# Lists of three groups made beside the scan, a term added by VectorE, and a check moved, in a four-layer graph network on one core

## The chip, the cores and the metric

The kernel runs on one core of a Trainium2 chip. The metric is the device time of one execution in microseconds (us). Five engines work from queues of their own, each strictly in order: TensorE (PE, matrix products), VectorE (DVE), ScalarE (ACT), GpSimd (POOL) and SyncE (SP, which here only starts transfers). They wait for one another through semaphores. Besides the engines 16 DMA engines move data; in this kernel SP starts the large transfers, and POOL the gathers, in which each of 128 partitions fetches a row or an element at an address of its own.

## The reference

A stack of four graph layers over 4096 nodes with 128 features each. `adj` is a 4096 x 4096 matrix that is mostly zeros: a diagonal, and off it entries of 0.05 to 1 with a probability that falls with the indices, so that the first rows and columns (the hubs) hold many more than the others.

```python
# h = relu(layernorm(x)) ahead of each layer; x = x + layer(h, adj) after it
L0: h @ W_self.T + (adj @ h) @ W_neigh.T + b
L1: h @ w[0] + (adj @ h) @ w[1] + (2 * adj @ (adj @ h) - h) @ w[2] + bias
L2: H = h @ weight.T                       # attention along adj.T
    C = alpha_src[None, :] + alpha_dst[:, None]
    Tau = adj.T * exp(max(0.2 * C, C))
    Z = (adj.T * (Tau / Tau.sum(axis=1, keepdims=True))) @ H
L3: s = h @ msg_w[:, :D].T
    d = h @ msg_w[:, D:].T
    messages = gelu(s[:, None, :] + d[None, :, :] + msg_b)
    aggregated = einsum('ijd,ij->id', messages, adj)
    new = concat([h, aggregated]) @ upd_w.T + upd_b
    g = gelu(new) + h
    out = layernorm(g) * ln_w + ln_b
```

Layer 3 needs one message per nonzero entry of `adj` and no more, since an entry of zero takes its message away.

## The kernel before

**Order of the work.** The kernel is written as tasks: Python generators that yield what they need next, an engine with a guessed duration (`yield "DVE", 0.35 * n`), a buffer out of a set (`yield banks`), or an event (`yield here[q]`). `Plan.run` goes through them at build time: it keeps a clock for each engine, takes the task that could begin first, among those within a short patience the one of the lowest rank, and emits its instructions. What it emits is the order of each engine's queue; on the chip the semaphores decide the times, and no engine overtakes in its queue. A guessed duration of PE is multiplied by `PE_TIME` = 0.72 before it is added to the clock. Where the planner sees a gap on PE it emits products of a tile of nothing (`fill`, L609), into a PSUM bank that is idle.

**Stages.** In the profiled execution: from 0 to about 373 us a *scan* reads all of `adj`, 128 rows at a time, and marks in bit masks which entries are nonzero (ACT makes an fp8 mask, DVE packs it into words and picks out candidates with `max8`); layer 0 runs beside it. Dense parts near the hubs are multiplied as whole blocks (`big`, L1138), the rest through rows that POOL gathers from tables in DRAM (`g`, L553) and PE multiplies (L1155). Layer 0's products end at 422 us. Layer 1 follows to 637, layer 2's first half to 904, the attention runs from 891 to 1245, layer 3 from there to 1524. `finish_0(g)` closes layer 0 for a group of 4 blocks of 128 rows (g from 0 to 7) and writes the next layer's input, a `norm`, into `hB[:, blocks, :128]`; hB has 32 x 130 columns.

**Lists of entries.** Layer 3 works on *chunks* of up to 128 nonzero entries, 158 in all, made by `entries(number, group)` for 11 groups of units. Group 0 is two hub units with 12 chunks; groups 1 and 2 have 7 each; groups 3 to 10 have 26, 22, 18, 16, 14, 12, 12 and 12. A pass waits for the scan's candidates of its units (`picked`), takes a lane of scratch tiles, decodes the bit marks on DVE, builds selection matrices (`selection`: ACT L622, DVE L624), multiplies them with the running counts (PE, L883 and L884), copies the product (ACT, `ehit`, L887), compares (DVE, L890) and unpacks row, column and address (`e_row`, `e_col`, `e_at`). Then it sets `decoded[number]`. `values()` waits for one group after the other and lets POOL gather the entries' values, one indirect DMA for each chunk (`e_val` from `adj`, L553). In the program before, these tasks are started when the scan is done (two lanes in the pool `second`); the first pass begins at 424.6 us, the last ends at 931.7; the first value gather is issued at 608.3, the last near 1170.

**Layer 3.** `Messages` has for each group g of 4 blocks a `prepare(g)` (own message of the diagonal), and for each batch of up to 4 chunks a `rows` task, which has POOL gather the rows of d (`m`, `tau` and `e` are the tiles' names, L553), and a `message` task: `selection` (L622, L624), the matrices r on DVE (L1400), a wait for the gathered rows, on PE a product of the identity with them (L1406, which adds d into PSUM) and products that add s (L1408), GELU from PSUM on ACT (L1412), and a product that sums into the accumulator (L1418). `finish(g)` makes the update, the layer norm (L1438 to L1459) and the last three DVE steps: times ln_w (L1463), plus ln_b (L1464), plus x (L1465), and has SP write the rows out.

**Check.** A dense version of the whole network stands behind the sparse one. After layer 3, written behind the last `plan.run()` and so behind everything in the queues, 79 small DVE instructions and one product (L1623 to L1646) look whether any list was too short for its entries; `n_bad` is loaded by every engine (L1648), and a branch (L1655) runs the dense version where it isn't 0. With these inputs it is 0.

Of the kernel before, what the change touches and what calls it, by code (L numbers as in the profile page):

```python
# [12 lines left out]
F32 = mybir.dt.float32  # L13
F8 = mybir.dt.float8e4
BF16 = mybir.dt.bfloat16
F16 = mybir.dt.float16
# [238 lines left out]
class Plan:  # L255
# [10 lines left out]
    PATIENCE = 0.3  # L266
    PE_TIME = 0.72
# [31 lines left out]
    def run(self, until=lambda: False):  # L299
        while self.tasks and not until():  # L300
# [32 lines left out]
            duration = want[1]  # L333
            if want[0] == "PE":
                duration *= self.PE_TIME
                gap = begin - self.free["PE"]
                if self.filler and gap > self.SHORT:
                    self.filler(self.free["PE"], gap * self.FILLED)
# [40 lines left out]
def sparse_stack(tc, x, adj, adjT, diag, w_self, w_neigh, b0, w1, b1, w2, att_src, att_dst,  # L379
# [8 lines left out]
    plan = Plan()  # L388
    EARLY = 7
    with ExitStack() as ctx:  # L390
# [7 lines left out]
        def kept(name, shape, dtype=F32):  # L398
            return keep.tile(list(shape), dtype, name=name, tag=name)
# [12 lines left out]
        def by_block(v, n):  # L412

            return v[:, None, :].to_broadcast([P, n, D])
# [189 lines left out]
        def fill(begin, time):  # L604

            idle = min((free, i, slots.items) for slots in (banks, picks) for free, i in slots.free + [(1e9, 0)])
# [198 lines left out]
        def entries(number, group):  # L805
# [178 lines left out]
        def finish_0(g, agg):  # L984
            blocks = slice(g * GB, (g + 1) * GB)
            rows = xN[:, blocks, :]
            p = yield banks
            yield "PE", 8 * 0.42
            times(p, GB, [(hT[:, g * BANK:(g + 1) * BANK], w_self_sb), (agg, w_neigh_sb)])
            plan.release(aggs, agg)  # L990
            yield on_dve(BANK)
            nc.vector.tensor_add(rows, rows, rows_of(p))
            plan.release(banks, p)
            yield from norm(blocks, hB[:, blocks, :D])
            h1_done[g].set(plan.finish)
# [320 lines left out]
        class Messages:  # L1316
# [37 lines left out]
            def prepare(self, g):  # L1354
# [34 lines left out]
                self.s_here[g].set(plan.finish)  # L1389

            def message(self, g, b, u, c, chunks, m, here):
# [7 lines left out]
                for q, k in enumerate(chunks):  # L1399
                    nc.vector.tensor_scalar(r[:, q, :], iota_row[:, :P], e_row[:, k:k + 1], e_val[:, k:k + 1],  # L1400
                                            op0=ALU.is_equal, op1=ALU.mult)
                for q in range(n):
                    yield here[q]
                p = yield banks
                yield "PE", n * 0.84
                nc.tensor.matmul(p[:, :n * D], ident, m[:, :n, :], start=True, stop=False)  # L1406
                for q in range(n):
                    nc.tensor.matmul(p[:, q * D:(q + 1) * D], lane["sel"][:, q, :], self.s_rows[g][:, b % GB, :],  # L1408
                                     start=False, stop=q == n - 1)
                plan.release(m_lanes, lane)  # L1410
                yield on_act(n * D, "gelu")
                nc.scalar.activation(m[:, :n, :], rows_of(p, n), AF.Gelu)  # L1412
                plan.release(banks, p)
# [11 lines left out]
            def finish(self, g):  # L1425
# [36 lines left out]
                yield "DVE", 2.1  # L1462
                nc.vector.tensor_mul(f, f, by_block(ln_w_sb, GB))  # L1463
                nc.vector.tensor_add(f, f, by_block(ln_b_sb, GB))  # L1464
# [23 lines left out]
        w02, w22, w2T, dst_w = (kept(k, (P, D)) for k in ("w02", "w22", "w2T", "dst_w"))  # L1488

# [30 lines left out]
        with tc.tile_pool(name="scan", bufs=1) as scanning:  # L1520
# [4 lines left out]
            words = scanning.tile([P, WORDS], I32, name="words", tag="words")  # L1525
            plan.filler = fill
# [12 lines left out]
            for s in COLS:  # L1539
                if s.cap:  # L1540
                    plan.start(col_flags(s), s.index * 1e-2 - 1.5)
            plan.start(fetch_columns(), 4)
            plan.run(lambda: layers[0].through.time is not None and all(p.time is not None for p in picked)
                     and len(rsegs.free) == len(rsegs.items))
# [3 lines left out]
        most = max(len(g.units) * (2 * g.width + 1) for g in GROUPS)  # L1548
        elanes = []
        for i in range(2):  # L1550
# [6 lines left out]
            n = max(sum(u.cap for u in g.units) for g in GROUPS)  # L1557
# [4 lines left out]
        for number, group in enumerate(GROUPS):  # L1562
            plan.start(entries(number, group), number * 1e-2 - 1)
        plan.start(values(), 6)
# [39 lines left out]
        with tc.tile_pool(name="lm", bufs=1, reuse_waits="tile") as lm:  # L1604
# [12 lines left out]
            picks.free = []  # L1617
            plan.run()


            bad = lm.tile([P, NPAIR + NU + 2], F32, name="bad", tag="bad")
            for i, item in enumerate(ROWS + COLS):
                nc.vector.tensor_scalar(bad[:, i:i + 1], pair_total[:, i:i + 1], float(item.cap * P), None, op0=ALU.is_gt)  # L1623
            for i, u in enumerate(UNITS):
                nc.vector.tensor_scalar(bad[:, NPAIR + i:NPAIR + i + 1], total[:, i:i + 1], float(u.places), None,
                                        op0=ALU.is_gt)
            nc.vector.tensor_reduce(bad[:, NPAIR + NU:NPAIR + NU + 1], over, axis=AX.X, op=ALU.max)

            count = lm.tile([P, NB], F32, name="count", tag="count")
            found = lm.tile([P, NB], F32, name="found", tag="found")  # L1630
            hub = sum(u.block == 0 for u in UNITS)
            nc.vector.tensor_reduce(count, marks.rearrange("p (b h) -> p b h", h=2), axis=AX.X, op=ALU.add)
            nc.vector.tensor_scalar(count, count, 2.0, float(-N), op0=ALU.mult, op1=ALU.add)
            nc.vector.tensor_scalar(found, diag_sb, 0.0, None, op0=ALU.is_gt)
            nc.vector.tensor_sub(count, count, found)
            nc.vector.tensor_reduce(found[:, 0:1], deg[:, :hub], axis=AX.X, op=ALU.add)
            nc.vector.tensor_copy(found[:, 1:], deg[:, hub:])
            nc.vector.tensor_tensor(count, count, found, op=ALU.not_equal)
            nc.vector.tensor_reduce(bad[:, NPAIR + NU + 1:], count, axis=AX.X, op=ALU.max)
            worst = lm.tile([P, 2], F32, name="worst", tag="worst")  # L1640
            nc.vector.tensor_reduce(worst[:, 0:1], bad, axis=AX.X, op=ALU.max)
            nc.vector.tensor_scalar(worst[:, 1:2], worst[:, 0:1], 0.0, None, op0=ALU.is_gt)
            p = accs.items[0]
            nc.tensor.matmul(p[:, :1], ones, worst[:, 1:2], start=True, stop=True)
            n_bad = kept("n_bad", (P, 1), I32)
            nc.vector.tensor_copy(n_bad, p[:, :1])  # L1646
# [340 lines left out]
```

## Time and profile before

| what | value |
|---|---|
| median of 6 runs | 1546.05 us (1537.2 to 1566.99) |
| profiled execution, its own time | 1550.04 us |
| its span, first to last instruction | 1547.9 us |
| mean granted clock of TensorE | 0.828 |
| list passes, first start to last end | 424.6 to 931.7 us |
| last DVE addition of layer 3 ends | 1523.88 us |
| n_bad ready | 1530.70 us |

The profile is one execution. A busy time is the sum of an engine's instructions, and an idle time in a group of instructions is the time just before them, with the work whose end released them behind an arrow. "remote" or "another core or an unknown queue" stands where the profile finds no sender for the signal that released an instruction; with one core there is no other core. Section 2 of the page cuts the span into 40 slices of 38.7 us, each digit a tenth of busy time. The chain of waits is followed back from the last instruction and adds up to the span, so it shows what set the end, while the busy shares show only how full each engine was.

### The profile page before, as it was taken

To read this page: it belongs to the slowest core of one execution; us is meant where nothing else is said; L and a number is where in the kernel's file an instruction comes from. 1 tells how busy PE (TensorE), PEld (TensorE's weight loads), DVE (VectorE), ACT (ScalarE), POOL (GpSimd) and SP (SyncE) were. 2 spreads that over 40 slices of the span, in tenths; PEclk is the share of its full clock that TensorE was granted. 3 is DMA by queue.
4 is the path that set the end of the run, shared out by engine and by line. 5 is a ranking of instruction groups with operands and counts; after the bars stand their busy time and mean duration, and the time that the engine had idled before them with its cause. 6 is when DMAs were issued, how large, how long until landed. Compare 5 with 4: busy or idle time off the path is not lost.

```text
span 1547.9 us, 19187 instructions
## 1 busy us (share of the span) xinstructions
PE 1069.0 (69%) x5943; PEld 731.5 (47%) x5943; DVE 794.5 (51%) x2982; ACT 671.0 (43%) x1344; POOL 766.1 (49%) x832
## 2 busy tenths in 40 slices
PE   6776778878568767557774288878676964677770
PEld 3444555554256555445553154434343633455660
DVE  5886557886366466345553155343343612244453
ACT  5984455763021212114352076556555711144463
POOL 4135554453455556645567525645566165564500
PEclk9897689897687889688887598878897986989885
DMA  8998889994366667755542043323333121121200
GB/s 257 352 332 295 280 269 344 330 332 144 99 188 186 192 203 218 231 152 158 148 120 84 17 126 102 91 86 90 90 87 105 54 54 42 42 55 46 62 19 16
DMA packets 175415, 236.03 MB, mean 152 GB/s; under 512 B 22452, under 2 KB 155336, under 8 KB 167112
## 3 DMA queue, kind: packets, MB, share of 16 engines
q1 hardware_dynamic: 148904, 186.45, 36.2%
q0 software_dynamic: 26400, 48.27, 12.4%
q8 instruction: 49, 0.80, 0.2%
q14 instruction: 62, 0.51, 0.1%
HBM read 203.41 MB, written 31.23 MB: 152 GB/s over the span
## 4 chain that ended last, share of the span: by engine, by line
PE 27%; another core or an unknown queue 12%; ACT 8%; issue 8%; DVE 5%; ACTq 0%; DMA 0%; POOL 0%; DVEq 0%; POOLq 0%
PE acc L1252 5%; PE acc L1254 5%; PE bank L597 3%; PE acc L1138 2%; PE acc L1418 2%; PE acc L1155 2%; PE bank L1408 1%; PE pick L609 1%; PE bank L1406 1%; ACT junk L1450 1%; PE bank L1276 1%; ACT e L1228 1%; ACT junk L568 1%; PE pick L1418 1%
## 5 line engine op out<-in xcount | busy, mean ns | idle before, releaser
L553 POOL DMA_INDIRECT e_val<-in_adj,e_at x158 | 155.4, 984 | 48.0 <-issue 45.6
L553 POOL DMA_INDIRECT g<-h_tab,fetch_row x136 | 135.5, 996 | 80.9 <-issue 34.3
L609 PE MATMUL pick<-nothing 128*128 128x512 f16 x532 | 145.0, 419 | 6.9 <-issue 6.7
L609 PEld LDWEIGHTS <-nothing 128*128 128x128 f16 x795 | 83.8, 108 | 104.3 <-issue 40.5
L553 POOL DMA_INDIRECT g<-a_tab,fetch_col x74 | 77.4, 1046 | 106.2 <-issue 45.8
L1138 PE MATMUL acc<-big,hA 128*128 128x256 f32 x448 | 123.8, 422 | 7.8 <-DMA big<-in_adjT 3.1
L553 POOL DMA_INDIRECT rseg<-in_adjT,seg_row x68 | 70.5, 1037 | 106.3 <-issue 29.2
L553 POOL DMA_INDIRECT cseg<-in_adj,seg_col x74 | 70.4, 951 | 67.4 <-issue 25.2
L1138 PEld LDWEIGHTS acc<-big,hA 128*128 128x128 f32 x448 | 91.6, 214 | 23.5 <-DMA big<-in_adjT 3.6
L1235 DVE TENSOR_TENSOR tau<-e,big 128x512 f32<-128x512 f32 (+3 forms) x61 | 54.3, 891 | 87.9 <-ACT e L1231 69.7
L553 POOL DMA_INDIRECT g<-u_tab,fetch_row x68 | 64.9, 955 | 65.7 <-PE acc L1155 39.9
L890 DVE SCALAR_TENSOR_TENSOR ehit<-ehit,pos,pick 128x32 f32<-128x32 f32 (+7 forms) x158 | 38.9, 286 | 110.9 <-ACT ehit L887 78.3
L1155 PE MATMUL acc<-big,g 128*128 128x256 f32 x272 | 85.9, 458 | 4.8 <-issue 3.2
L553 POOL DMA_INDIRECT tau<-d_tab,e_col x63 | 60.2, 956 | 57.1 <-PE acc L1418 15.9
L553 POOL DMA_INDIRECT m<-d_tab,e_col x70 | 67.8, 969 | 40.2 <-issue 16.8
L768 ACT ACTIVATE mask<-dst 128x2048 fp8e4<-128x2048 f32 x43 | 81.8, 1902 | 9.1 <-DMA dst<-in_adj 4.8
L887 ACT COPY ehit<-pick 128x192 f32<-128x192 f32 (+7 forms) x74 | 20.5, 288 | 148.7 <-remote 60.0
L622 ACT ACTIVATE sel_t<-iota_row,mids 128x512 f32<-128x512 f32 (+3 forms) x43 | 27.1, 642 | 126.3 <-DVE mids L617 101.8
L568 ACT ACTIVATE junk<-xN,stat 128x128 f32<-128x128 f32 x128 | 51.4, 401 | 68.7 <-DVE stat L564 23.4
L609 PE MATMUL bank<-nothing 128*128 128x512 f16 x263 | 73.1, 424 | 0.4 <-DVE s L1369 0.4
L883 PE MATMUL pick<-eA,esel 128*128 128x65 f16 (+7 forms) x158 | 27.5, 249 | 58.7 <-DVE esel L624 23.2
L1155 PEld LDWEIGHTS acc<-big,g 128*128 128x128 f32 x272 | 60.0, 232 | 16.1 <-issue 6.0
(328 smaller groups left out, 2744.4 us busy)
## 6 DMA issues: line engine op xcount, KB each, us to landing
dst<-in_adj SPq DMA_DIRECT2D x43, 1024.0 KB
big<-in_adjT SPq DMA_DIRECT2D x45, 512.0 KB
raw<-in_adj SPq DMA_DIRECT2D x21, 1024.0 KB
big<-in_adjT SPq DMA_DIRECT2D x66, 256.0 KB
big<-r_tab SPq DMA_DIRECT2D x30, 512.0 KB
c_tab<-cseg SPq DMA_DIRECT2D x74, 128.0 KB
r_tab<-rseg SPq DMA_DIRECT2D x68, 128.0 KB
big<-c_tab SPq DMA_DIRECT2D x15, 512.0 KB
```

The lines of the kernel that those rows point to most:

```text
L553: nc.gpsimd.indirect_dma_start(out=dst, out_offset=None, in_=table[:, :], in_offset=bass.IndirectOffsetOnAxis(ap=index, axis=0))
L568: nc.scalar.activation(junk, src[:, k, :], AF.Square, bias=st[:, 0, k:k + 1], accum_out=st[:, 1, k:k + 1])
L597: nc.tensor.matmul(p[:, k * D:(k + 1) * D], lhs[:, k * P:(k + 1) * P], w, start=i == 0, stop=i == len(terms) - 1)
L609: nc.tensor.matmul(idle[2][idle[1]], nothing[:, :P], nothing, start=True, stop=True)
L768: nc.scalar.activation(mask[:, h * HALF:(h + 1) * HALF], raw_of[b, h], AF.Sigmoid, scale=1e38, accum_out=marks[:, 2 * b + h:2 * b + h + 1] ...
L890: nc.vector.scalar_tensor_tensor(hit[:, q, :], hit[:, q, :], pos0[:, k + q:k + q + 1], pv[:, q, W:2 * W], op0=ALU.is_le, op1=ALU.mult, acc ...
L1138: nc.tensor.matmul(acc, self.near[:, b, :D], as_rows(t)[:, k, :], start=count == 0, stop=count == every - 1)
L1155: nc.tensor.matmul(acc, row[:, :D], r, start=count == 0, stop=count == every - 1)
L1235: nc.vector.tensor_mul(tau[:, :n, :], e[:, :n, :], a[:, :n, :])
L1252: nc.tensor.matmul(acc[0:1, CS:2 * CS], parts[k][:, D + 1:], tau[:, k, :], start=False, stop=False)
L1254: nc.tensor.matmul(acc[:, :CS], parts[k][:, :D], e[:, k, :], start=False, stop=self.count[s.index] == every - 1)
L1418: nc.tensor.matmul(acc[:, b % GB * P:(b % GB + 1) * P], m[:, q, :], r[:, q, :], start=False, stop=all(self.left[g * GB + k] == 0 for k in ...
```

## The change

Four things are changed, in one diff.

- `entries` takes its lanes as an argument. The passes of groups 0, 1 and 2, and `values()`, are started within the scan, at ranks -5 and 6 (the scan itself has -4). They share one lane, of which part is the upper part of hB that layer 0 has not yet written; so `finish_0` waits, for a group whose blocks reach into that scratch, for the three passes. With widths as they are this holds for groups 4 to 7. The scan's `run` goes on until the three are decoded.
- In `message` the identity product goes. s is multiplied into PSUM first, without waiting for the gathered rows; then DVE adds PSUM to the gathered rows in SBUF, and GELU reads SBUF. There are 49 such batches.
- The check becomes a task (`missing`) started beside layer 3 at rank 9, with `n_bad` allocated ahead; ln_b is added to x in `prepare` and no longer at the end.
- `DVE_TIME = 0.9` multiplies the guessed durations of DVE in the planner. (The changed key in `fill` only keeps a tie from being compared further.)

```diff
+    DVE_TIME = 0.9
     PE_TIME = 0.72
...
+            if want[0] == "DVE":
+                duration *= self.DVE_TIME
...
+    EARLY_GROUPS = 3
...
-        def entries(number, group):
+        def entries(number, group, elanes):
...
@@ finish_0
+            if blocks.stop * (D + 2) > hub_scratch:
+                for d in decoded[:EARLY_GROUPS]:
+                    yield d
             yield from norm(blocks, hB[:, blocks, :D])
...
@@ Messages.prepare
                 self.s_here[g].set(plan.finish)
+                yield on_dve(BANK)
+                nc.vector.tensor_add(xN[:, blocks, :], xN[:, blocks, :], by_block(ln_b_sb, GB))
...
@@ Messages.message
+                p = yield banks
+                yield "PE", n * 0.42
+                for q in range(n):
+                    nc.tensor.matmul(p[:, q * D:(q + 1) * D], lane["sel"][:, q, :], self.s_rows[g][:, b % GB, :],
+                                     start=True, stop=True)
+                plan.release(m_lanes, lane)
                 for q in range(n):
                     yield here[q]
-                p = yield banks
-                yield "PE", n * 0.84
-                nc.tensor.matmul(p[:, :n * D], ident, m[:, :n, :], start=True, stop=False)
-                for q in range(n):
-                    nc.tensor.matmul(p[:, q * D:(q + 1) * D], lane["sel"][:, q, :], self.s_rows[g][:, b % GB, :],
-                                     start=False, stop=q == n - 1)
-                plan.release(m_lanes, lane)
+                yield on_dve(n * D)
+                nc.vector.tensor_add(m[:, :n, :], m[:, :n, :], rows_of(p, n))
+                plan.release(banks, p)
                 yield on_act(n * D, "gelu")
-                nc.scalar.activation(m[:, :n, :], rows_of(p, n), AF.Gelu)
-                plan.release(banks, p)
+                nc.scalar.activation(m[:, :n, :], m[:, :n, :], AF.Gelu)
...
@@ Messages.finish
-                yield "DVE", 2.1
+                yield "DVE", 1.4
                 nc.vector.tensor_mul(f, f, by_block(ln_w_sb, GB))
-                nc.vector.tensor_add(f, f, by_block(ln_b_sb, GB))
                 nc.vector.tensor_add(f, f, xN[:, blocks, :])
...
+        def missing():
+            bad = lm.tile([P, NPAIR + NU + 2], F32, name="bad", tag="bad")
...
+            p = yield banks
+            yield on_pe(2)
+            nc.tensor.matmul(p[:, :1], ones, worst[:, 1:2], start=True, stop=True)
+            yield "DVE", 0.2
+            nc.vector.tensor_copy(n_bad, p[:, :1])
+            plan.release(banks, p)
...
@@ the scan's pool
+            flat, at, lane = hB.rearrange("p b d -> p (b d)"), NB * (D + 2), {}
+            for k, width in [(k, -(-most // 2) + 2 * GB) for k in ("et", "ev", "epop", "ecum", "evf")] + [("t", BANK)]:
+                at -= width
+                lane[k] = flat[:, at:at + width]
...
+            early_lanes, hub_scratch = Slots([lane]), at
...
+            for number in range(EARLY_GROUPS):
+                plan.start(entries(number, GROUPS[number], early_lanes), number * 1e-2 - 5)
+            plan.start(values(), 6)
             plan.run(lambda: layers[0].through.time is not None and all(p.time is not None for p in picked)
-                     and len(rsegs.free) == len(rsegs.items))
+                     and len(rsegs.free) == len(rsegs.items)
+                     and all(d.time is not None for d in decoded[:EARLY_GROUPS]))
...
         for number, group in enumerate(GROUPS):
-            plan.start(entries(number, group), number * 1e-2 - 1)
-        plan.start(values(), 6)
+            if number >= EARLY_GROUPS:
+                plan.start(entries(number, group, elanes), number * 1e-2 - 1)
...
@@ after layer 3
+            n_bad = kept("n_bad", (P, 1), I32)
+            plan.start(missing(), 9)
             plan.run()
-            bad = lm.tile([P, NPAIR + NU + 2], F32, name="bad", tag="bad")
...
```

More of the change, by code (lines that the diff above doesn't have):

```diff
@@ L604, in fill @@
         def fill(begin, time):
-            idle = min((free, i, slots.items) for slots in (banks, picks) for free, i in slots.free + [(1e9, 0)])
+            idle = min(((free, i, slots.items) for slots in (banks, picks) for free, i in slots.free + [(1e9, 0)]),
+                       key=lambda slot: slot[:2])
             if idle[0] < begin - 1.0:
@@ L1488, in sparse_stack @@
         w02, w22, w2T, dst_w = (kept(k, (P, D)) for k in ("w02", "w22", "w2T", "dst_w"))
+        def missing():
+            bad = lm.tile([P, NPAIR + NU + 2], F32, name="bad", tag="bad")
+            limits = [(pair_total[:, i:i + 1], float(item.cap * P)) for i, item in enumerate(ROWS + COLS)]
+            limits += [(total[:, i:i + 1], float(u.places)) for i, u in enumerate(UNITS)]
+            for i, (have, most) in enumerate(limits):
+                if i % 8 == 0:
+                    yield "DVE", 0.5
+                nc.vector.tensor_scalar(bad[:, i:i + 1], have, most, None, op0=ALU.is_gt)
+            yield "DVE", 0.5
+            nc.vector.tensor_reduce(bad[:, NPAIR + NU:NPAIR + NU + 1], over, axis=AX.X, op=ALU.max)
+            count = lm.tile([P, NB], F32, name="count", tag="count")
+            found = lm.tile([P, NB], F32, name="found", tag="found")
+            hub = sum(u.block == 0 for u in UNITS)
+            nc.vector.tensor_reduce(count, marks.rearrange("p (b h) -> p b h", h=2), axis=AX.X, op=ALU.add)
+            nc.vector.tensor_scalar(count, count, 2.0, float(-N), op0=ALU.mult, op1=ALU.add)
+            yield "DVE", 0.6
+            nc.vector.tensor_scalar(found, diag_sb, 0.0, None, op0=ALU.is_gt)
+            nc.vector.tensor_sub(count, count, found)
+            nc.vector.tensor_reduce(found[:, 0:1], deg[:, :hub], axis=AX.X, op=ALU.add)
+            nc.vector.tensor_copy(found[:, 1:], deg[:, hub:])
+            yield "DVE", 0.9
+            nc.vector.tensor_tensor(count, count, found, op=ALU.not_equal)
+            nc.vector.tensor_reduce(bad[:, NPAIR + NU + 1:], count, axis=AX.X, op=ALU.max)
+            worst = lm.tile([P, 2], F32, name="worst", tag="worst")
+            nc.vector.tensor_reduce(worst[:, 0:1], bad, axis=AX.X, op=ALU.max)
+            nc.vector.tensor_scalar(worst[:, 1:2], worst[:, 0:1], 0.0, None, op0=ALU.is_gt)
+            p = yield banks
[4 more added lines that the diff above has]
+            plan.release(banks, p)
         making = ctx.enter_context(ExitStack())
@@ L1525, in sparse_stack @@
             words = scanning.tile([P, WORDS], I32, name="words", tag="words")
+            most = max(len(g.units) * (2 * g.width + 1) for g in GROUPS[:EARLY_GROUPS])
+            n = max(sum(u.cap for u in g.units) for g in GROUPS[:EARLY_GROUPS])
+            flat, at, lane = hB.rearrange("p b d -> p (b d)"), NB * (D + 2), {}
+            for k, width in [(k, -(-most // 2) + 2 * GB) for k in ("et", "ev", "epop", "ecum", "evf")] + [("t", BANK)]:
+                at -= width
+                lane[k] = flat[:, at:at + width]
+            for k, width in (("eA", most), ("eB", -(-most // 2))):
+                lane[k] = scanning.tile([P, width], F16, name=f"{k}_0", tag=f"{k}_0")
+            for k, width in [("first", GB), ("ehit", BANK)] + [
+                    (k, n) for k in ("dv", "da", "db", "dr", "dat", "dbit0", "dbit1", "dbit2", "dbit3", "dcol", "drow")]:
+                lane[k] = scanning.tile([P, width], F32, name=f"{k}_0", tag=f"{k}_0")
+            lane["sel"] = scanning.tile([P, GB, P], F16, name="esel_0", tag="esel_0")
+            early_lanes, hub_scratch = Slots([lane]), at
             plan.filler = fill
@@ L1547, in sparse_stack @@
         h2s = tiles(second, "h2", 2, (P, GB, D))
-        most = max(len(g.units) * (2 * g.width + 1) for g in GROUPS)
+        most = max(len(g.units) * (2 * g.width + 1) for g in GROUPS[EARLY_GROUPS:])
         elanes = []
-        for i in range(2):
+        for i in range(1, 3):
             def lane_tile(name, width, dtype=F32):
@@ L1556, in sparse_stack @@
                          "sel": second.tile([P, GB, P], F16, name=f"esel_{i}", tag=f"esel_{i}")})
-            n = max(sum(u.cap for u in g.units) for g in GROUPS)
+            n = max(sum(u.cap for u in g.units) for g in GROUPS[EARLY_GROUPS:])
             for k in ("dv", "da", "db", "dr", "dat", "dbit0", "dbit1", "dbit2", "dbit3", "dcol", "drow"):
@@ L1617, in sparse_stack @@
             picks.free = []
+            n_bad = kept("n_bad", (P, 1), I32)
+            plan.start(missing(), 9)
             plan.run()
-            bad = lm.tile([P, NPAIR + NU + 2], F32, name="bad", tag="bad")
[L1622 to L1646, printed above, removed]
         in_order(tc)
```

## The prediction, made before the changed kernel ran

> **What bounds the kernel now.** Read first on the page: busy shares, the 40 slices, the engine line of the chain.
>
> ```profile
> PE 1069.0 (69%) x5943; PEld 731.5 (47%) x5943; DVE 794.5 (51%) x2982; ACT 671.0 (43%) x1344; POOL 766.1 (49%) x832
> ...
> DVE  5886557886366466345553155343343612244453
> ...
> DMA  8998889994366667755542043323333121121200
> ...
> PE 27%; another core or an unknown queue 12%; ACT 8%; issue 8%; DVE 5%; ACTq 0%; DMA 0%; POOL 0%; DVEq 0%; POOLq 0%
> ```
>
> No engine is full. Transfers run at 8 to 9 tenths for the first ten slices (0 to 387 us, the scan with layer 0) and never again. 12% of the chain is "unknown": an engine waits for a signal whose sender the profile cannot name. The table by stretches (columns: PE, PEld, DVE, ACT, POOL busy us with counts, clock, DMA share, GB/s) says where that lies:
>
> ```profile
> 0.00:100.00 100.00, 74.98 (x499) 42.37 (x500) 74.38 (x243) 79.76 (x155) 27.74 (x85) 0.91 0.91 309
> 100.00:200.00 100.00, 69.11 (x502) 48.55 (x502) 64.40 (x195) 47.79 (x70) 60.50 (x58) 0.77 0.85 295
> 200.00:300.00 100.00, 81.77 (x622) 56.66 (x621) 70.20 (x190) 63.38 (x97) 43.28 (x42) 0.89 0.89 310
> 300.00:373.00 73.00, 57.38 (x450) 36.63 (x448) 55.32 (x168) 41.81 (x66) 37.05 (x35) 0.86 0.79 273
> 821.00:878.00 57.00, 10.27 (x39) 6.71 (x39) 11.13 (x73) 8.71 (x22) 43.05 (x46) 0.57 0.14 40
> 1245.00:1300.00 55.00, 22.74 (x93) 13.84 (x92) 4.95 (x14) 2.41 (x4) 35.47 (x38) 0.66 0.20 52
> 1300.00:1400.00 100.00, 70.01 (x396) 54.57 (x395) 33.44 (x100) 28.95 (x60) 59.55 (x62) 0.88 0.18 46
> ```
>
> From 821 to 878 everything but POOL stands still. The groups of that stretch:
>
> ```profile
> L553 POOL DMA_INDIRECT e_val<-in_adj,e_at x43 | 40.7, 947 | 13.1 <-issue 12.8 <-DMA e_val<-in_adj,e_at 0.3
> ...
> L887 ACT COPY ehit<-pick 128x96 f32<-128x96 f32 x3 | 0.7, 232 | 28.2 <-remote 27.2 <-PE acc L1138 1.0
> ...
> L890 DVE SCALAR_TENSOR_TENSOR ehit<-ehit,pos,pick 128x32 f32<-128x32 f32 x9 | 1.7, 244 | 26.9 <-ACT ehit L887 26.9
> ```
>
> ACT's copy waits 27.2 us for a matmul that PE had finished; it goes when POOL's 43 back-to-back value gathers end. The stretch from 1245 is the same, with 36 gathers of layer 3. So a long unbroken run of gathers costs about its own length, 0.947 + 0.3 = 1.25 us a gather, on every engine. That is my reading of these rows, not proved.
>
> **The lists and values moved early.** 26 of the 158 chunks (three of eleven lists, 664 of 2064 list columns) leave the time after the scan. All entries lines (L807 to L929) hold 224.6 us of DVE, 85.6 of PE and 21.3 of ACT; three lists are 16% by chunks to 32% by columns, so DVE 37 to 72, PE 14 to 27, ACT 3.5 to 7.
>
> What they gain later, by the built issue order: the long run falls from 43 to 37 value gathers: 6 x 1.25 = -7.5 (bounds 0 to -7.5). In the attention 58 stand on POOL instead of 80. There the chain, asked stretch by stretch, has 22 us of unknown waits (930 to 1150); 22/80 of it is -6. Bounds: 0 if PE (180.5 busy of 235) sets the pace, -20 if most of 22 x 1.25 = 27.5 comes off. Layers 1 and 2 keep as many gathers (74 for 78) but lose a sixth of the decoding; a sixth of the 30.5 unknown us of 640 to 830 is -5 (0 to -20).
>
> What they cost in the scan: DVE holds 264 of 373 us, and becomes 301 to 336, 81 to 90%. The lists have a rank ahead of the scan of marks, so the marks wait behind list pieces of 1 to 2 us; behind the marks wait the mask buffers, and behind these SP's reads of adj. POOL gets 26 x 1.25 = 32 us more (now 169 of 373), in queue order among layer 0's row gathers: while a value gather waits for its list, these stand too. The second half of layer 0's normalizations (groups 4 to 7) now waits for the three lists, because their scratch is the upper part of hB. Four of the first ten slices have DVE at 8 tenths; work spread evenly puts 0.4 x 54 = 22 us there, and what is idle in them is about as much. I take a third of the 22, +8. Bounds: 0, DVE's 109 idle us hide it all and transfers still end the scan; +45, the middle of 37 to 72 with a sixth hidden.
>
> A rule speaks against this part. The Trainium skill, "SBUF — State Buffer", section "Who interferes with whom": VectorE and GpSimd share a port pair, a VectorE tensor_scalar in a two-port mode holds it for the whole instruction, and descriptors of a GpSimd DMA cannot be written meanwhile. The trace leans that way: row gathers take 1037 ns in the scan (DVE 71% busy) and value gathers 947 in the 821 stretch (DVE 20%). By the rows, 26 x 0.09 = 2.3 us of POOL; by the rule, if each of the scan's 154 gathers met one more 0.25 us instruction, an estimate of 39 us on POOL.
>
> **d added by VectorE.** Rows of 1245 to 1524:
>
> ```profile
> L1406 PE MATMUL bank<-tau,ident 128*128 128x512 f32 (+2 forms) x28 | 13.3, 561 | 1.0 <-issue 1.0
> ...
> L1412 ACT ACTIVATE tau<-bank 128x512 f32<-128x512 f32 (+2 forms) x14 | 6.8, 500 | 80.8 <-remote 66.1 <-PE bank L1408 9.4 <-issue 5.3
> ...
> L1464 DVE TENSOR_TENSOR f<-f,ln_b_sb 128x512 f32<-128x512 f32 x8 | 5.5, 693 | 0.3
> ...
> L1438 DVE TENSOR_TENSOR f<-bank,upd_b_sb 128x512 f32<-128x512 f32 x6 | 4.1, 691 | 11.4 <-PE bank L1408 7.0 <-PE bank L597 4.4
> ```
>
> 49 identity products go: all L1406 records are 98 passes, 46.2 us of PE. 49 adds come, of which 23 are 512 wide, 19 are 384, 2 are 256, 5 are 128; the nearest row is L1438, one operand in PSUM, 0.691 at 512. By width: 23 x 0.69 + 19 x 0.52 + 2 x 0.35 + 5 x 0.18 = 27.4 (33.8 if width saved nothing). DVE is a third busy there. The wait for the gather moves from PE to DVE, where the next batch's r (L1400) and msel (L624) are queued behind it; PE's selecting products run ahead. On the chain L1406 into a bank is 1%, some 15 us, a third of its busy time. The same third of the adds is 9: -6. Bounds: -15 (adds wholly hidden) to +13 (all 27.4 on the path). GELU from SBUF: L1441 0.630 against 0.59 from PSUM, 49 x 0.04 = 2 us on an ACT that is 29% busy: nothing. If ACT were the bound, 2.
>
> ln_b is added in prepare, under the gathers; the last group's path loses one 0.69: -0.7 (its bounds are 0 and that).
>
> **The check.** End of the chain now:
>
> ```profile
> 1523.19 0.69 DVE f L1465
> 1523.88 1.94 DVE bad L1623 x32
> 1525.82 2.12 DVE bad L1625 x35
> ```
>
> It ends with n_bad at 1530.70: 6.8 us after the last add. Then all engines load n_bad and branch, resuming at 1534.2 to 1535.7, and POOL has still to do this:
>
> ```profile
> L1655 POOLq INC_SWDGE_SEM  x1: 2500/2500/2500, 1535.1 to 1535.1; - x1
> ...
> L1982 POOLq DRAIN  x3: 46/103/9460, 1537.6 to 1547.6; - x3
> ```
>
> From last add to end: 1547.9 - 1523.9 = 24.0. With the check beside layer 3's start (79 small DVE instructions in the stretch where DVE has 5 of 55 us; uncovered they cost their 6.8), n_bad is known long before. POOL's last gather starts near 1472, so its branch, the 2.5 and the 9.5 can lie under the last 50 us. Left after the last add: load, branch and resume 4 to 5 on DVE, ACT, SP, beside them the output's landing, then 1 to 2 of barriers: 6.5, so -17.5. If the drain starts only when all is done, -6.8. I take -15, near the long end, since nothing that POOL waits for there comes late.
>
> **VectorE at 0.9** changes the planner's guesses, so every engine's order, and nothing in the work. Fillers fall from 795 to 732 for the same reason. No row prices an order; I take 0, and +-10, the size of one gather run of eight either way.
>
> **Sum.** -15 - 0.7 - 6 - 6 - 7.5 - 5 + 8 = -32. The profiled execution took 1550.0 (span 1547.9 and 2.1 around it): 1518. It is 4 above the median of six, 1546, so in their terms **1514**.
>
> **Rivals.** *The scan becomes the loss (slower).* Mechanism: list pieces on DVE's queue delay the marks, POOL's value gathers wait for lists with row gathers queued behind, and groups 4 to 7 wait for hB. For it: DVE 74 and 70 us of 100 already, and SP already waits 72.0 us for ACT's masks in the scan. Against: transfers bound the stage at 0.79 to 0.91, and DVE's sum still fits. It decides once the scan loses over 40; at +60, just past its bound of 45, and all else as above, 1546 - 40 + 60 = 1566. *Only the tail comes.* The chain's other waits are of POOL's runs, and a run of 37 may stall as one of 43; layer 3's adds neutral, scan +8: 1546 - 15.7 + 8 = 1538; without the scan's loss 1530. For it: the 36-gather run after the attention is untouched. *More than I counted:* -17.5, -15 and half of the other two long bounds, scan 0: 1546 - 17.5 - 0.7 - 15 - 7.5 - 10 - 10 = 1485. For it: PE loses 46 us in a stage where it is 70% busy.
>
> **Numbers.** Likeliest (1495 to 1530) 0.56; scan loss 0.20; tail only 0.14; more 0.10. A measurement tells about 0.5%, 8 us, from no change. Faster: 0.56 + 0.10 + 0.10 of tail only = 0.76. Within: 0.04 + 0.04 of the scan case = 0.08. Slower: 0.16. The range takes in the larger gain whole and the scan case up to a loss of 45 or so: 1480 to 1555.
>
> **What would show it.** Right: the last add to the end in 6 to 9 us; layer 0's last product no later than 430; a stall of some 46 us, not 56, after layer 2's last row gathers; no L1406 on the chain, PE still waiting "remote" after 1245 of the old time. Wrong: layer 0 ending past 460 with DVE over 90% and DMA below 0.8; DVE waiting for layer 3's gathers with PE waiting for r; POOL's drain still last by 9 us.

## The result: 1.3% slower

| | before | changed | ratio, 95% interval |
|---|---|---|---|
| median, us | 1551.66 (69 runs, 1530.19 to 1577.66) | 1564.44 (32 runs, 1551.66 to 1584.62) | 1.0129 [1.0109, 1.0149] |

Faster was forecast, by 2%. Here and below a median is of all runs, while a ratio leaves out runs over 1.5% above the fastest of the same kernel. The profiled execution of the changed kernel has a span of 1550.8 us, only 2.9 more than that of the kernel before; its time, 1552.6, lies at the low end of its range. A later pair of traces, taken beside one another (before_again and after_again), differs by 26. Both pairs tell the same by stages, except for layers 1 and 2. Layers 0 to 2 end here where ScalarE's last copy of their accumulator starts (L1164 before, L1172 now), the attention with its last product (L1254, L1262):

| stage, us | before | changed | before_again | after_again | mean difference | forecast |
|---|---|---|---|---|---|---|
| scan and layer 0 | 421.6 | 476.3 | 423.5 | 478.8 | +55.0 | +8 |
| layers 1 and 2 | 482.6 | 471.8 | 479.0 | 485.3 | -2.3 | -12.5 |
| attention | 322.0 | 302.6 | 313.8 | 304.4 | -14.4 | -6 |
| layer 3, to the last addition | 297.7 | 294.2 | 300.2 | 292.5 | -5.6 | -6.7 |
| last addition to the end | 24.0 | 5.9 | 24.2 | 5.9 | -18.2 | -15 |

One row is far off, the first, and it decides. The page of the changed kernel:

```profile
PE 1038.6 (67%) x5782; PEld 718.3 (46%) x5782; DVE 815.3 (53%) x3031; ACT 676.4 (44%) x1346; POOL 760.2 (49%) x832
...
DVE  5896668777737654664631103452443571426663
...
DMA  8997967766654466776465303341333312111210
...
PE 26%; another core or an unknown queue 12%; issue 8%; DVE 8%; ACT 6%; DMA 1%; POOL 1%; SPq 0%; DVEq 0%; ACTq 0%; POOLq 0%
```

Before, the transfers stood at 8 and 9 tenths for nine slices; now they stand at 6 and 7 from the sixth on, and drag on to the eleventh. DVE has no slice over 8 tenths after the third, so it is not simply full. The scan's middle and end, from 140 us until the last `max8`, is one line of the table by stretches for each kernel (PE, PEld, DVE, ACT, POOL busy us, clock, DMA share, GB/s). Kernel before:

```profile
140.00:357.00 217.00, 171.84 (x1338) 118.21 (x1336) 157.55 (x432) 128.34 (x193) 109.52 (x105) 0.85 0.86 297
```

Changed kernel:

```profile
140.00:409.00 269.00, 187.61 (x1382) 129.93 (x1381) 199.50 (x666) 138.20 (x224) 139.37 (x135) 0.78 0.73 246
```

DVE does 42 us more there, and the stretch is 52 longer. Its idle time was 59 before and is 70 now: taken as a whole, the added work went into none of it. What ended the idle time before, the six longest of that stretch (engine, tile and line, what it waited for: us in all, times, longest):

```profile
DVE pf L701 <- remote: 14.7, 6, 6.9
DVE xN L992 <- PE acc L1138: 9.4, 2, 7.9
DVE hit L659 <- remote: 7.9, 1, 7.9
DVE xN L992 <- PE acc L1155: 4.7, 1, 4.7
DVE pst L640 <- PE bank L638: 3.9, 2, 2.5
DVE hit L659 <- PE pick L656: 3.2, 6, 1.0
```

These six are 44 of the 59 us: waits for TensorE's products, or for signals whose sender the profile does not find.

The end went as forecast. The moved control work of POOL (the columns: operation, count, shortest/median/longest ns, first and last start):

```profile
L1692 POOLq COMPARE_BRANCH  x1: 58/58/58, 1485.3 to 1485.3; - x1
L1692 POOLq INC_SWDGE_SEM  x1: 2476/2476/2476, 1493.6 to 1493.6; - x1
...
L2019 POOLq DRAIN  x3: 46/103/9378, 1496.1 to 1550.5; - x3
```

The branch stands at 1485, the 9.4 us drain at 1496, both under layer 3; the chain's last work is `1544.25 0.69 DVE f L1475`, which ends 5.9 us before the end.

### The profile page after: what moved, and what is told of

Its sections match the earlier page's. It is cut to its first block, busy times and chain, and to the rows that moved or that the text cites. A ratio compares the mean times of both kernels' runs of the same rounds, so it can differ in the third digit from the quotient of the medians.

```text
span 1550.8 us, 18964 instructions
## 1 busy us (share of the span) xinstructions
PE 1038.6 (67%) x5782; PEld 718.3 (46%) x5782; DVE 815.3 (53%) x3031; ACT 676.4 (44%) x1346; POOL 760.2 (49%) x832
## 4 chain that ended last, share of the span: by engine, by line
PE 26%; another core or an unknown queue 12%; issue 8%; DVE 8%; ACT 6%; DMA 1%; POOL 1%; SPq 0%; DVEq 0%; ACTq 0%; POOLq 0%
PE acc L1262 4%; PE acc L1260 4%; PE acc L1146 3%; PE bank L601 3%; PE acc L1163 2%; PE acc L1429 2%; PE pick L614 1%; PE bank L614 1%; PE bank L1415 1%; DVE r L1410 1%; ACT junk L1461 1%; PE pick L1429 1%; ACT junk L572 1%; DVE ehit L895 1%
## 5 line engine op out<-in xcount | busy, mean ns | idle before, releaser
L1146 PE MATMUL acc<-big,hA 128*128 128x256 f32 x448 | 138.1, 449 | 46.8 <-DMA big<-in_adjT 29.9
L1146 PEld LDWEIGHTS acc<-big,hA 128*128 128x128 f32 x448 | 96.7, 227 | 68.9 <-DMA big<-in_adjT 34.2
L614 PEld LDWEIGHTS <-nothing 128*128 128x128 f16 x732 | 79.2, 110 | 106.3 <-issue 51.2
L614 PE MATMUL pick<-nothing 128*128 128x512 f16 x415 | 112.3, 415 | 12.8 <-issue 12.5
L892 ACT COPY ehit<-pick 128x96 f32<-128x96 f32 (+9 forms) x74 | 20.4, 287 | 179.1 <-remote 55.1
L614 PE MATMUL bank<-nothing 128*128 128x512 f16 x317 | 97.8, 455 | 0.0
L1163 PE MATMUL acc<-big,g 128*128 128x256 f32 x272 | 78.6, 423 | 10.8 <-issue 8.1
L1410 DVE TENSOR_SCALAR r<-iota_row,e_row,e_val 128x128 f32<-128x128 f32 x158 | 46.8, 352 | 63.7 <-remote 39.8
L557 POOL DMA_INDIRECT tau<-d_tab,e_col x53 | 50.7, 958 | 38.3 <-PE acc L1429 14.6
```

The lines of the kernel that those rows point to most:

```text
L557: nc.gpsimd.indirect_dma_start(out=dst, out_offset=None, in_=table[:, :], in_offset=bass.IndirectOffsetOnAxis(ap=index, axis=0))
L1146: nc.tensor.matmul(acc, self.near[:, b, :D], as_rows(t)[:, k, :], start=count == 0, stop=count == every - 1)
L1163: nc.tensor.matmul(acc, row[:, :D], r, start=count == 0, stop=count == every - 1)
```

## The experiments

Five sets of runs, each with the kernel before beside it; ratios are to that. They did not all fall on the same chip: sets 1 and 2 ran on one where the kernel before takes 1502 and 1560 us, sets 3 to 5 on three others, where it takes 1196 to 1198. That difference is larger than anything studied here, so kernels are compared within a set, or by ratios. In set 1 the kernel before was 3.7% faster than in set 2 on the same chip, and why stays open; so set 1's ratios are taken as too high, and its traces are used more than its times.

Changes are to the changed kernel. All keep the moved check and ln_b. Each variant also gets an order of its own from the planner, for all queues. Every trace is one execution.

| kernel | lists, values | scale | d added by | ratio, 95% interval (set) |
|---|---|---|---|---|
| changed, after_again, after_3 | early, early | 0.9 | DVE | 1.0129 [1.0109, 1.0149]; 1.0085 [1.0042, 1.0127] (2); 1.0044 [1.0011, 1.0077] (4) |
| late_values, _2 | early, late | 0.9 | DVE | 1.0264 [1.0080, 1.0447] (1); 1.0050 [1.0019, 1.0081] (4) |
| late_lists, _2, _3 | late, late | 0.9 | DVE | 1.0292 [1.0106, 1.0477] (1); 1.0038 [1.0008, 1.0068] (3); 1.0013 [0.9986, 1.0041] (4) |
| marks_first, _2 | behind the marks | 0.9 | DVE | 0.9942 [0.9876, 1.0007] (1); 1.0097 [1.0062, 1.0132] (3) |
| dve1, _2 | early, early | 1.0 | DVE | 1.0338 [1.0126, 1.0549] (1); 1.0187 [1.0144, 1.0229] (5) |
| marks_dve1 | behind the marks | 1.0 | DVE | 1.0186 [1.0134, 1.0239] (3) |
| late_dve1, _2, _3 | late, late | 1.0 | DVE | 0.9755 [0.9681, 0.9829] (2); 0.9867 [0.9821, 0.9913] (3); 0.9835 [0.9768, 0.9901] (4) |
| check_only, _2 | late, late | 1.0 | PE | four runs, 1507, 1513, 1538 and 1552, against 1560.11, no ratio (2); 0.9856 [0.9814, 0.9899] (5) |

### Set 1: which part holds up the scan

late_lists (and later _2, _3). With the lists the scratch lane in hB goes too, and so finish_0's wait for them:

```diff
-    EARLY_GROUPS = 3
+    EARLY_GROUPS = 0
...
-            for number in range(EARLY_GROUPS):
-                plan.start(entries(number, GROUPS[number], early_lanes), number * 1e-2 - 5)
-            plan.start(values(), 6)
...
+        plan.start(values(), 6)
```

> All three early lists and all value gathers are started after the scan again, as before the change; the added d on VectorE, the moved check, ln_b and VectorE at 0.9 stay. If the early lists and their gathers are what holds up the scan (marks last at 408 us instead of 357), the marks end at 357 +- 10 again, layer 0's last product copy is back near 422 (476 in the changed kernel), and the ratio to the kernel before falls from 1.013 to 0.975 to 0.99, depending on how much of the 37 us that layer 2 and the attention had gained is lost. If the reordering by VectorE at 0.9 is the cause, the marks still end past 390 and the ratio stays over 1.005.

late_values (and _2), where the lists stay early:

```diff
                 plan.start(entries(number, GROUPS[number], early_lanes), number * 1e-2 - 5)
-            plan.start(values(), 6)
...
                 plan.start(entries(number, group, elanes), number * 1e-2 - 1)
+        plan.start(values(), 6)
```

> The three lists are decoded beside the scan, but their 26 value gathers come after it. Theory A (gathers): the value gathers fill the pauses between the row gathers, runs get longer, and TensorE's signals arrive late; then the marks end at 357 to 370, as without early lists. Theory B (lists): the passes themselves, their round trips over VectorE, TensorE and ScalarE and the wait of groups 4 to 7, hold the queues; then the marks end at 390 to 408 as in the changed kernel and the ratio stays 1.005 to 1.015.

marks_first:

```diff
-                plan.start(entries(number, GROUPS[number], early_lanes), number * 1e-2 - 5)
+                plan.start(entries(number, GROUPS[number], early_lanes), number * 1e-2 - 3)
```

> The lists keep their place in the scan but rank behind the marks (-3 in place of -5). Theory B in the form that list pieces stand ahead of marks on VectorE's queue: the marks end at 360 to 375, ratio 0.985 to 0.995. If it is not the rank but the round trips and the gathers: marks still past 390, ratio 1.005 to 1.015.

dve1:

```diff
-    DVE_TIME = 0.9
+    DVE_TIME = 1.0
```

> The changed kernel with VectorE counted at 1.0 by the planner. If the scale is the cause of the loss: marks near 360, ratio below 0.99. If it only shuffles: marks 395 to 420, ratio 1.003 to 1.023.

In the traces the scan answers clearly. late_lists:

```profile
140.00:362.00 222.00, 170.66 (x1317) 116.17 (x1318) 153.14 (x427) 126.78 (x191) 113.19 (x110) 0.85 0.86 298
```

late_values:

```profile
140.00:379.00 239.00, 181.52 (x1415) 129.65 (x1414) 198.46 (x661) 137.05 (x223) 111.52 (x108) 0.83 0.82 276
```

Without early lists the marks end at 362, as before the change. The decoding alone puts 45 us on DVE and moves the end by 17: there the idle time did take some of it (41 left of 69). The value gathers put nothing on DVE, 28 us on POOL, and move the end by another 30, to 409. So on this chip the gathers are the larger part, as far as one trace of each order can tell (with set 4, below). dve1 (marks until 415, layer 0 until 472) says that the scale is not what slows the scan. marks_first has its marks at 376, just past the upper edge of what was expected. The times of the four answer less well: only marks_first came out near its expected ratio (0.9942). late_lists and late_values did not come out below the changed kernel's, against what I expected of their scans, in the set whose kernel before was out of line. The traces show one reason. What late_lists wins in the scan and layer 0, 46 us (430.4 against 476.3), it gives back for the most part: its layers 1 and 2 take 489.9 (471.8 in the changed kernel) and its attention 324.3 (302.6), and its span is 1544.7 against 1550.8.

Where the gathers act is seen in layer 0's own addition (`xN`, in finish_0), on DVE ahead of the next marks. In the changed kernel, 140 to 409:

```profile
L997 DVE TENSOR_TENSOR xN<-xN,bank 128x512 f32<-128x512 f32 x6 | 4.1, 685 | 20.1 <-remote 16.2 <-PE bank L601 3.8
```

In late_values, 140 to 379:

```profile
L997 DVE TENSOR_TENSOR xN<-xN,bank 128x512 f32<-128x512 f32 x6 | 4.1, 684 | 5.1 <-PE bank L601 5.1
```

With value gathers among the row gathers, DVE stands 15 us longer there, mostly for signals without a sender ("remote"), with marks behind it in the queue. That is half of the 29 us by which DVE's idle time differs (70 against 41).

Two other paths were open. A value gather that waits for its list holds up the row gathers behind it on POOL; in the changed kernel, from the start to 409, the wait for lists (L931) is 8.2 us of the idle time at value gathers:

```profile
L557 POOL DMA_INDIRECT e_val<-in_adj,e_at x26 | 25.5, 979 | 17.9 <-DVE e_at L931 8.2 <-issue 6.9 <-DVE hit L664 2.8
```

And group 4's norm waits for the three lists. From its addition to its norm that is 320.2 to 367.7 us in the changed kernel, but 289.3 to 360.9 in late_values, where layer 0 is done 37 us sooner. So by this row the first explains 8.2 of the 30 us at most, and the second wait is longer where the scan is shorter.

### Set 2: the parts that are left, and both kernels on one chip

late_dve1 is late_lists with the scale taken back:

```diff
-    DVE_TIME = 0.9
+    DVE_TIME = 1.0
```

check_only is late_dve1 with the old message, L1406 back on PE and GELU from PSUM:

```diff
-                yield "PE", n * 0.42
+                yield "PE", n * 0.84
+                nc.tensor.matmul(p[:, :n * D], ident, m[:, :n, :], start=True, stop=False)
...
-                yield on_dve(n * D)
-                nc.vector.tensor_add(m[:, :n, :], m[:, :n, :], rows_of(p, n))
+                yield on_act(n * D, "gelu")
+                nc.scalar.activation(m[:, :n, :], rows_of(p, n), AF.Gelu)
...
-                nc.scalar.activation(m[:, :n, :], m[:, :n, :], AF.Gelu)
```

after_again and before_again are the two kernels unchanged.

> Of the change only the check as a task beside layer 3 and ln_b added in prepare are left: lists and values after the scan, d added by TensorE, VectorE counted at 1.0. If the parts of the change add up, the end after the last addition falls from 24 to 6 us and the ratio to the kernel before is 0.985 to 0.99, the rest of the trace standing as before. If moving the check cost something (new order of layer 3, a bank taken), the ratio is over 0.995.

> As check_only, and d is added by VectorE: lists and values after the scan, VectorE at 1.0. If VectorE's addition helps or is neutral, the ratio is 0.975 to 0.99; if it is the part that made late_lists 1.03, layer 3 (last attention product to last addition) is longer than 300 us and the ratio is over 1.01. If instead the scale 0.9 made late_lists slow, this is 0.975 to 0.99 while late_lists was 1.03.

> The changed kernel unchanged, to have its trace and time on the chip of the runs beside it: ratio 1.011 to 1.015 if the ratio doesn't depend on the chip; marks end near 408 us, layer 0 near 476.

> The kernel before unchanged, for its trace on this chip: ratio 1; marks end near 357, layer 0 near 422, layer 2 near 904, attention near 1226, last addition near 1524, each scaled by this chip's time over 1550.

late_dve1 is 2.45% faster than the kernel before, and 52 us below after_again by medians. Its layer 3 took 278.5 us (300.2 in before_again), its end 5.8, its scan and layer 0 430.1. So VectorE's addition and the moved check together cost nothing, and the loss is in early lists and scale together. How it splits between these two is not measured in time on this chip, since no set there has the changed kernel and late_lists beside one another. Nothing shows that VectorE's addition earned anything either: two of check_only's runs, at 1507 and 1513, are no slower than late_dve1's 1512 to 1521. after_again is 0.85% slower than the kernel before, below the 1.1 to 1.5% I expected, with the marks at 412 and layer 0 at 479.

### Set 3: the scale, and lists behind the marks

late_lists_2, late_dve1_2 and marks_first_2 are repeats; marks_dve1 is marks_first with `DVE_TIME = 1.0`.

> marks_first again, beside the kernel without early lists. VectorE works on 37 us of lists beside the scan in the changed kernel, and its idle time between 140 us and the end of the marks did not shrink (60 before, 70 after). If the loss is this work standing ahead of the marks, the marks end at 370 to 380 again (408 to 412 in the changed kernel) and the ratio is 0.985 to 1.0.

> Lists behind the marks and VectorE counted at 1.0. If the scale 0.9 costs time in itself, this is 1 to 2% below marks_first_2; if it only gives another order, within 1% of it on either side.

> All lists after the scan, scale 0.9: 1.029 in the first set, whose runs of the kernel before were 3% faster than elsewhere. If the scale 0.9 costs time, it is 2% or more above late_dve1_2 beside it; if the first set's kernel before was the odd one, it is 0.975 to 0.995 and within 1% of late_dve1_2.

> All lists after the scan, scale 1.0, check moved, d on VectorE: 0.9755 before. Again 0.968 to 0.983 if the ratio holds from set to set.

With late lists the scale 0.9 costs 1.7% (1.0038 against 0.9867). With lists behind the marks it earns 0.9% (1.0097 against 1.0186). A cause of its own would hardly change its sign: the scale gives another order of every queue, and which order is the better seems to depend on the rest. For late lists I had expected either 2% and more or less than 1%; it is neither. late_dve1_2, at 0.9867, lies just above the range expected. Lists behind the marks are no way out: marks_first_2 has its marks at 330 (325 in late_lists_2), sooner than expected, but its ratio is above the expected 0.985 to 1.0: what is put off lands in layer 1, 191 us against 171.

### Set 4: side by side at one scale

> The changed kernel, as the measure for the three beside it: ratio 1.005 to 1.015 on a chip where the kernel before takes about 1550 us, 1.01 to 1.03 on one where it takes about 1200.

> Lists and values after the scan, all else as in the changed kernel. If the early lists are the loss, this is 1.5 to 3% below after_3 (the scan with layer 0 45 to 50 us shorter, layer 2 and the attention 20 to 35 us longer). If it is not below after_3, the loss is elsewhere.

> Lists beside the scan, their value gathers after it. If the gathers are the larger part of the loss, this is 1 to 2.5% below after_3, with the marks ending at 375 to 385 where after_3 has 408; if the decoding alone is the loss, within 0.7% of after_3.

> Lists and values after the scan and VectorE at 1.0. If the scale 0.9 costs time where lists are late, this is 1 to 2% below late_lists_3 again, ratio 0.97 to 0.99; if the difference of the earlier sets was chance, within 0.7% of it.

On this chip the early lists cost next to nothing at 0.9: after_3 1202.88, late_values_2 1202.00, late_lists_3 1199.38 us. My expectation of 1.5 to 3% missed, and after_3's ratio is below the expected 1.01 to 1.03. The scan tells why. late_lists_3:

```profile
140.00:328.00 188.00, 162.14 (x1273) 110.58 (x1271) 148.51 (x405) 123.25 (x187) 112.64 (x109) 0.87 0.96 343
```

late_values_2:

```profile
140.00:346.00 206.00, 163.92 (x1317) 114.96 (x1314) 190.27 (x635) 130.64 (x213) 108.01 (x106) 0.86 0.88 311
```

after_3:

```profile
140.00:344.00 204.00, 162.34 (x1299) 114.12 (x1299) 191.09 (x639) 129.88 (x212) 137.14 (x133) 0.86 0.90 312
```

The decoding moves the end by 18, as on the other chip; DVE is now busy 191 of 204, so here it is nearly full. (Without early lists transfers fill the stretch, at 0.96.) The 29 us more of gathers on POOL move it by -2, where they had cost 30. And layer 0's addition doesn't wait in after_3:

```profile
L997 DVE TENSOR_TENSOR xN<-xN,bank 128x512 f32<-128x512 f32 x6 | 4.1, 681 | 1.7 <-PE bank L601 1.7
```

Layer 2 then gives back 15 (155.1 against 170.0), and the sum is next to nothing. The scale was again worth 1.8% with late lists: late_dve1_3 1178.83.

### Set 5: the last two parts

> Only the check and ln_b are moved. The tail alone is worth 18 us: ratio 0.985 to 0.99 on either kind of chip if the rest stands still. Against late_dve1 (0.9755 on one chip, 0.984 to 0.987 on two others) it tells what VectorE's addition is worth: over 0.99 on a chip of the second kind, and the addition earns 0.5% or more; 0.984 to 0.988, and it earns nothing.

> Early lists with their values, VectorE at 1.0. If the early lists are a loss at this scale too, this is 1% or more above late_dve1's ratio: over 0.995 on a chip of the fast kind (0.984 to 0.987 there without early lists), over 1.0 on the slower one; if within 0.5% of it, the early lists cost nothing at 1.0.

check_only_2 came out at 0.9856, between the ratios of late_dve1 on chips of the same kind (0.9835 and 0.9867). So VectorE's addition earns nothing that can be measured there, and the moved check with ln_b earns all of it: 1.44% of 1196 is 17 us, about the 18 by which the tail shrank on the first chip. dve1_2 at 1.0187 puts the early lists at 1.0 some 3.2 to 3.5% above late_dve1 on such chips; its marks end at 367 where late_dve1_3 has 316. It is also 1.4% above the changed kernel of set 4 (1.0044): with early lists the scale 0.9 was the better one, across two sets and two chips of that kind. So at 1.0 the early lists cost over 3% there, and at 0.9 next to nothing.

late_dve1 beats the kernel before in each of three sets, and the changed kernel in the two sets that have it (2 and 4); check_only does as well with less.

## Why the prediction was wrong, point by point

**The scan (+8, bounds 0 to +45) was the step that failed; it was +55.** The work was sized well: 37 to 72 us of DVE were forecast, and 45 were added until the marks' end. What it costs was not, in two terms. The decoding was to cost 8: what fell into slices with room was put at nothing, and of the 22 us in full slices a third was charged. late_values against late_lists has 17. And the 26 value gathers, 32 us of POOL by the prediction's own working, had no term in the sum at all; the changed kernel against late_values has 30. The other 5 to 9 us stand in late_lists too, beside the kernel before.

For the decoding I set 54 us against "DVE's 109 idle us". But that idle time was mostly waits for TensorE or for signals without a sender, in a queue that doesn't overtake. A list piece behind such a wait doesn't use it; only pieces that the order happens to put ahead of one do. The runs show it from both sides: decoding filled 28 of the 69 idle us of late_lists, and on the chip of set 4, with 40 idle us and none of them "remote", 24, until DVE was busy for 190 of 206.

For the gathers there was a price that I did give, in the wrong place: value gathers among the row gathers lengthen the stretches in which signals come late. I had read that from the stalls at 821 and 1245 and priced it as gain (gathers taken out of a run) but not as loss (gathers put into one). That the changed kernel, with its gathers, has its marks 30 us later than late_values is shown, by one trace of each. That it is the gathers and not the other order is supported by set 4, where the same two orders differ by -2. That it is through late signals is argued, from L997's rows (half of the idle time) and from set 4, where there are no late signals and no cost.

Two readings were off besides. The page has transfers at 8 to 9 tenths for nine slices, not ten. And the chain of waits doesn't add up to the span: in the kernel before it begins at 597 us and so covers 61% of it; nothing on it could price the scan.

The rival that I gave 0.20 to named this place, and put the point of decision at a loss of over 40; the loss was 55 and the gains 40 together. Of the signs of being wrong, layer 0 past 460 and DMA below 0.8 came (476, and 0.73 from 140 on), DVE over 90% did not (199.5 of 269 us).

**Layers 1 and 2 (-12.5): -2.3.** Layer 2 gained 12 in the mean (17.6 and 5.5), which goes with the lists that were ready earlier: late_lists, without them, has 277.8 there against the changed kernel's 249.6. Layer 1 lost 9 (6.8 and 11.8), which I had not counted and did not trace to a cause. The long run fell from 43 to 37 as the order said, but at its end nine more values follow four memsets, and the stall goes on through them. From 870 to 932, in the columns of the table by stretches:

```profile
870.00:932.00 62.00, 20.51 (x72) 12.04 (x72) 1.49 (x7) 7.38 (x17) 47.26 (x52) 0.63 0.14 41
```

DVE works 1.5 us in 62, and the 2 us of memsets did not end the stall.

**Attention (-6): -14.4**, within its bounds of 0 to -20. It has fewer value gathers, as forecast (49 in place of 69 in the first pair of traces), but that they are the cause is not shown: late_values has 70 there and took 298.6, no longer than the changed kernel's 302.6, and check_only, with 69, took 308.4.

**d on VectorE (-6): no gain that any time shows.** Layer 3 was 5.6 shorter, but check_only, where TensorE adds d, has 292.9, as short as the changed kernel's 294.2; so that layer 3 came out near its -6.7 is luck. late_dve1's trace has 278.5, 14 less than check_only's, but its attention is 8 longer and its time no shorter. On the other kind of chip layer 3 took 220.5 in check_only_2 and 222.0 in late_dve1_3. The 49 additions took 28.2 us (27.4 forecast, by width). Rows from 1250 to 1545:

```profile
L1410 DVE TENSOR_SCALAR r<-iota_row,e_row,e_val 128x128 f32<-128x128 f32 x147 | 43.7, 353 | 61.8 <-remote 39.8 <-PE acc L1429 6.5 <-issue 5.6
...
L1421 DVE TENSOR_TENSOR m<-m,bank 128x512 f32<-128x512 f32 (+2 forms) x15 | 8.8, 597 | 0.3 <-issue 0.3
```

DVE hardly stood in front of the addition (0.3 us in this group, 4 in all of them), though the wait for the gathers is now there. DVE stands at r instead, 61.8 us (39.8 of it for signals without a sender), where the same row of the kernel before, from 1245 to 1524, had 16.7 (10.9).

**The check (-15): -18.2**, just past its bound of -17.5, by the mechanism that was named. The tail is 6 to 7 us in every trace with the moved check, and it is the only part whose gain held on both kinds of chip.

**VectorE at 0.9 (0, +-10): too narrow.** 1.7% with late lists, -0.9% with lists behind the marks, -1.4% with early lists (across two sets): -17 to +21 us of 1200. It is a draw of orders, and I treated a draw as nothing.

**The rule on the shared port** (the Trainium skill, "SBUF — State Buffer", "Who interferes with whom") would have put 39 us on POOL by the estimate then made. This case does not show it: the scan's 125 gathers of rows and segments (g, rseg) took 130.1 us on POOL before the change and 129.3 after it, with 45 us more of DVE beside them. On the chip of set 4, where DVE's share from 140 to the last mark rose from 79% to 94%, such a gather took 1035 ns in late_lists_3 and 1041 in after_3.

## What to carry to other kernels

Before work is moved into an engine's idle time, look at what ends that idle time: in an in-order queue a wait for another engine is not room by itself, and the work adds to the length unless it can stand ahead of the wait. When a change also shifts a planner's guesses, run it once with the guesses as they were; here that draw was as large as the change. And split a bundle: the check and ln_b alone were a gain of 1.4% where that was measured, and the bundle was a loss, of 0.4% on a chip of that kind and 1.3% on the first.

## What was not expected of the hardware

I had read from the trace that a long run of gathers holds up every other engine by about its own length. It looks so on one chip and not on others. On the chip of sets 1 and 2 TensorE itself crawls in such a run. Timeline of the changed kernel, whose times are like those of that chip (start, duration, engine, line; the idle time before it in brackets):

```profile
908.87 0.58 PE L1146 MATMUL acc<-big,hA 128*128 128x256 f32 x1 [2.21 <-issue]
909.95 0.95 POOL L557 DMA_INDIRECT e_val<-in_adj,e_at  x1 [0.30 <-issue]
910.27 0.10 PEld L614 LDWEIGHTS <-nothing 128*128 128x128 f16 x1 [2.51 <-issue]
911.21 0.95 POOL L557 DMA_INDIRECT e_val<-in_adj,e_at  x1 [0.30 <-issue]
911.68 0.58 PE L614 MATMUL pick<-nothing 128*128 128x512 f16 x1 [2.22 <-issue]
```

It takes one instruction in 1.4 us, with nothing to wait for that the profile shows, beside a gather every 1.25 us; the median of such products (L614) takes 0.38 in the whole trace. On the chip of set 4 POOL of late_dve1_3 has 174 instructions in 233 us of the attention, nearly all gathers and one behind the other, and PE works all the while:

```profile
727.00:960.00 233.00, 213.67 (x952) 120.26 (x950) 126.47 (x267) 164.85 (x336) 180.42 (x174) 0.96 0.42 112
```

Its chain, over the whole span, has no unknown waits at all, where before_again has 18% over the whole span, and after_again 13% from 589 us on:

```profile
DMA 27%; PE 27%; DVE 14%; ACT 13%; POOL 10%; issue 8%; SPq 1%; POOLq 0%; DVEq 0%; ACTq 0%
```

The same kernel before takes 1196 to 1198 us there and 1502 to 1560 on the first. TensorE's granted clock differs too, 0.63 in the stretch from 870 and 0.96 in this one; which follows from which is not shown. What makes the one chip's signals late stays open: no run paced the gathers of such a run or took them away to see the signals return, and it may lie outside the program.
